# Attention weights turned by VectorE, a mask in the scores' tile shape, and queries and keys copied out of PSUM by ScalarE, with a new order of steps

## The chip, the cores and the metric

The kernel runs on one core of a Trainium2 chip. A core has a matrix engine (TensorE, PE in the profile, with PEld for its weight loads), VectorE (DVE), ScalarE (ACT), GpSimd (POOL) and a queue engine for DMAs (SyncE, SP). Each engine takes its instructions in order; semaphores tie them together. The metric is the device time in microseconds. The kernel before was run three times: 4847.99, 4833.86 and 4830.67 us, median 4833.86 us.

## The reference

The model is computed in float32 on 16 sequences of 256 tokens with 128 features. It has four parts in a row:

- latent attention (16 heads of 8), added to the stream;
- six layers of windowed attention with a feed-forward part; window 32, 16 heads of 64;
- a state-space layer (a scan over chunks);
- two layers of windowed attention with a feed-forward part; window 64, 8 heads of 64.

One layer of windowed attention, cut to what matters here:

```python
q, k, v = split(x @ Wqkv)                     # per head, 64 wide
q = l2norm(q) * q_scale ; k = l2norm(k) * k_scale
q = q * cos * scale + rotate_half(q) * sin * scale
k = k * cos / scale + rotate_half(k) * sin / scale
sim = einsum(q, [k of the window before, k of this window]) * 8.0
sim = where(mask, -max, sim)
out = softmax(sim) @ [v of the window before, v of this window]
x = x + out @ Wo
x = x + (a * gelu(gate)) @ W2 + b2            # a, gate = layernorm(x) @ W1 + b1
```

## The kernel before

The windowed layers are one class, Pipeline, used twice: W = 32 for the six layers and W = 64 for the two. The residual stream stays in SBUF as `k.y`, features on partitions. The work is cut into blocks of 128 tokens, 32 blocks per layer; two blocks make a sequence (a pair), and four blocks make a tile of 512 tokens for the feed-forward part. So the six-layer stage has 192 blocks, 96 pairs and 48 tiles.

What a block goes through, by step names. `project` (L791) multiplies y by Wqkv into PSUM (`pq`, `pk`, 128 tokens by 1024). `square` (L804, ACT) and `squares` (L847, DVE) give the norms. `cosine` (L817) and `sine` (L827), both on DVE, multiply the PSUM result by the tables into SBUF (`rot`, `t2`). `rotate` (L855, POOL) adds the two. `pair_newton` (L859, POOL) makes the reciprocal roots of a pair's norms in 13 small instructions, and `unit` (L874, POOL) applies them. `turn` (L881, PE) transposes to PSUM and `keep` (L888, ACT) copies to SBUF. `hide` (L970, PE) writes the mask into the bank of the scores as a product of two small matrices, `score` (L988, PE) adds q by k there in tiles of 64 rows by 32 columns. `maximum`, `subtract` (DVE), `exp` (ACT), `total`, `invert` (DVE) and `divide` (L1035, POOL) are the softmax. `turn_p` (L1040, PE) transposes the weights by 128x128 pieces and `keep_p` (L1046, ACT) copies them out.

For W = 32 the value and output matrices are folded into one (`wvo`), so the weights are applied to y itself. `turn_y` (L923) transposes the block of y, `keep_y` (L942, ACT) copies it, `spread` (L958) copies it by DMAs on SP's queue into four shifted windows `vc`, and `gather` (L1076, PE) multiplies windows by weights. `keep_u` (L1093, ACT) copies to `oT`, `pair_output` (L1103, PE) multiplies by `wvo` once per pair in four parts, and `pair_add` (L1115, DVE) adds to y. Steps named `ff_` are the feed-forward part, once per tile.

The order is written out by hand in PLAN32 and PLAN64 (L532, L549). An entry `name@lag` says that in round i the step is issued for block i - lag; the rounds run in `run` (L756), and each engine's queue gets its instructions in that order. So a waiting instruction holds everything that stands behind it on its engine. Before each round one piece of foreign work is issued: `rest`, the end of the stage before, and two hooks. PSUM is used as four double banks of 128x1024 float32, called q, s, t and o. The second string of a plan gives each tile its double bank; a new tile waits until the last user of that bank has been read.

## Time and profile before

The table is from the profile of one execution. The page gives its span, 4843.4 us, and no other time of its own; the span stands 0.2% above the median of the three runs.

| | value |
|---|---|
| span of the profiled execution | 4843.4 us |
| first stage, latent attention | until 440 us |
| six-layer stage | 440 to about 3740 us |
| state-space stage | until about 4080 us |
| two-layer stage | to the end |
| busy share PE / DVE / ACT / POOL | 94% / 70% / 57% / 68% |
| granted TensorE clock, mean | 0.975 |

In a line of a group, the shapes come first, then the number of instructions, the busy time in us and the mean duration of one in ns; behind the second bar stands the idle time of the engine just before them and what ended it. A line of the timeline begins with start and duration in us. A line about one source line gives the shortest, median and longest duration in ns. In the windows view a line gives the stretch, its length, the busy time of PE, PEld, DVE, ACT and POOL (with the number of instructions), the granted clock, the share of DMA and its rate. TensorE handles a float32 matrix product as two records.

### The profile page before, as it was taken

To read this page: it belongs to the slowest core of one execution; us is meant where nothing else is said; L and a number is where in the kernel's file an instruction comes from. 1 tells how busy PE (TensorE), PEld (TensorE's weight loads), DVE (VectorE), ACT (ScalarE), POOL (GpSimd) and SP (SyncE) were. 2 spreads that over 40 slices of the span, in tenths; PEclk is the share of its full clock that TensorE was granted. 3 is DMA by queue.
4 is the path that set the end of the run, shared out by engine and by line. 5 is a ranking of instruction groups with operands and counts; after the bars stand their busy time and mean duration, and the time that the engine had idled before them with its cause. 6 is when DMAs were issued, how large, how long until landed. Compare 5 with 4: busy or idle time off the path is not lost.

```text
span 4843.4 us, 121146 instructions
## 1 busy us (share of the span) xinstructions
PE 4566.5 (94%) x50834; PEld 3046.7 (63%) x50834; DVE 3371.6 (70%) x4050; ACT 2746.6 (57%) x3412; POOL 3302.7 (68%) x3603
## 2 busy tenths in 40 slices
PE   7896899999999999999999999999998998999998
PEld 4553566666666666666666666666665665566665
DVE  4664777777777777777777777777673775788774
ACT  3553465566656666566665666656664553566554
POOL 2444677777777777777777777777874354777774
PEclk9997999999999999999999999999998898999999
DMA  1111010001100010001000010000011000111111
GB/s 35 35 32 43 16 39 16 16 16 23 34 16 21 17 40 16 16 17 39 17 16 16 17 39 17 16 16 24 23 25 33 24 10 18 58 43 44 49 57 39
DMA packets 208039, 131.52 MB, mean 27 GB/s; under 512 B 61260, under 2 KB 179416, under 8 KB 207496
## 3 DMA queue, kind: packets, MB, share of 16 engines
q1 hardware_dynamic: 197096, 118.78, 9.9%
q8 instruction: 403, 6.60, 0.6%
q0 software_dynamic: 8704, 4.48, 0.5%
q14 instruction: 140, 1.15, 0.1%
q10 hardware_dynamic: 1696, 0.51, 0.0%
HBM read 29.65 MB, written 8.39 MB: 8 GB/s over the span
## 4 chain that ended last, share of the span: by engine, by line
PE 71%; DVE 16%; POOL 5%; ACT 4%; issue 2%; SPq 1%; DMA 0%; DVEq 0%; ACTq 0%; POOLq 0%
PE py L1111 13%; PE pq L796 7%; PE hid L1168 6%; PE u L1085 6%; PE scores L998 5%; PE pk L796 5%; PE tq L886 4%; DVE n L853 3%; PE tp L1044 3%; PE fy L1202 3%; PE tk L886 2%; DVE rotq L821 2%; PE st L383 2%; POOL rstd L116 1%; DVE rotk L821 1%
## 5 line engine op out<-in xcount | busy, mean ns | idle before, releaser
L1111 PE MATMUL py<-oT,wvo 128*128 128x256 f32 x3072 | 679.0, 379 | 1.2 <-ACT oT L1098 1.2
L1038 POOL TENSOR_TENSOR pr<-pr,rs 128x1024 f32<-128x1024 f32 x256 | 490.2, 1915 | 271.5 <-DVE rs L1033 231.8
L857 POOL TENSOR_TENSOR rotq<-rotq,t2q 128x1024 f32<-128x1024 f32 x256 | 605.6, 2366 | 36.1 <-DMA w<-in_L_ffn_W 23.6
L1111 PEld LDWEIGHTS py<-oT,wvo 128*128 128x128 f32 x3072 | 576.2, 190 | 76.0 <-ACT oT L1098 1.6
L1098 ACT COPY oT<-u 128x1024 f32<-128x1024 f32 x384 | 377.2, 1015 | 315.4 <-PE u L1085 306.9
L796 PE MATMUL pq<-wqkv,y 128*128 128x512 f32 x1024 | 493.1, 604 | 25.5 <-DMA wqkv<-in_L_ffn_Wqkv 14.0
L877 POOL TENSOR_TENSOR rotq<-rotq,rn 128x1024 f32<-128x1024 f32 x256 | 489.5, 1912 | 11.2
L101 DVE TENSOR_TENSOR y<-y,py 64x256 f32<-64x256 f32 x256 | 107.3, 419 | 525.0 <-PE py L1111 523.3
L821 DVE TENSOR_TENSOR rotq<-pq,tab 128x1024 f32<-128x1024 f32 x256 | 313.4, 1224 | 220.7 <-ACT sqq L807 169.5
L903 ACT COPY qT<-tq 128x1024 f32<-128x1024 f32 (+1 forms) x256 | 230.8, 902 | 412.1 <-PE tq L886 412.1
L857 POOL TENSOR_TENSOR rotk<-rotk,t2k 128x1024 f32<-128x1024 f32 x192 | 454.5, 2367 | 0.0
L998 PEld LDWEIGHTS scores<-kT,qT 64*32 64x32 f32 (+1 forms) x26624 | 321.4, 107 | 159.8 <-issue 96.7
L1029 DVE TENSOR_REDUCE rs<-pr 128x16 f32<-128x1024 f32 (+1 forms) x256 | 312.4, 1220 | 156.7 <-ACT pr L1022 151.9
L807 ACT ACTIVATE sqq<-pq 128x1024 f32<-128x1024 f32 x256 | 262.2, 1024 | 262.7 <-PE pq L796 244.9
L1085 PE MATMUL u<-prT,vc 64*128 64x256 f32 x3072 | 404.4, 394 | 2.3 <-DVE t2k L833 0.3
L998 PE MATMUL scores<-kT,qT 64*32 64x64 f32 (+2 forms) x26624 | 399.8, 224 | 4.7 <-ACT kT L903 2.8
L796 PE MATMUL pk<-wqkv,y 128*128 128x512 f32 x768 | 393.4, 601 | 0.0
L1168 PE MATMUL hid<-fxn,w 128*128 128x512 f32 (+1 forms) x768 | 388.3, 617 | 4.9 <-DVE ga L1190 2.7
L866 POOL TENSOR_SCALAR rn<-n 128x64 int32<-128x64 int32 (+1 forms) x128 | 30.5, 238 | 518.8 <-DVE n L853 518.8
L877 POOL TENSOR_TENSOR rotk<-rotk,rn 128x1024 f32<-128x1024 f32 x192 | 365.9, 1906 | 0.1
L1022 ACT ACTIVATE pr<-pr 128x1024 f32<-128x1024 f32 x256 | 270.6, 1057 | 135.3 <-DVE pr L1014 128.0
L1009 DVE TENSOR_REDUCE nm<-scores 128x16 f32<-128x1024 f32 (+1 forms) x256 | 311.9, 1218 | 21.0 <-PE scores L998 19.7
(285 smaller groups left out, 9772.0 us busy)
## 6 DMA issues: line engine op xcount, KB each, us to landing
vc<-vt SPq DMA_DIRECT2D x1152, 32.0 KB
vc<-vt SPq DMA_DIRECT2D x64, 256.0 KB
vc<-vt SPq DMA_DIRECT2D x96, 128.0 KB
vc<-vt SPq DMA_DIRECT2D x576, 16.0 KB
wqkv<-in_L_ffn_Wqkv SPq DMA_DIRECT2D x12, 512.0 KB
x<-xd SPq DMA_DIRECT2D x23, 256.0 KB
xd<-x SPq DMA_DIRECT2D x22, 256.0 KB
wo<-in_L_ffn_Wo SPq DMA_DIRECT2D x6, 512.0 KB
```

What stands on the lines that cost most here:

```text
L796: self.nc.tensor.matmul(pq[:, 512 * int(half) : 512 * int(half) + 512], self.k.y[:, b, c0 : c0 + P], L.wqkv[:, col : col + 512], start=Tru ...
L821: self.nc.vector.tensor_mul(rot.rearrange("p (w h) e -> p w h e", w=ways), self.get(n, "p" + group).rearrange("p (w h e) -> p w h e", w=wa ...
L857: self.nc.gpsimd.tensor_add(rot, rot, self.done(n, "t2" + group))
L877: self.nc.gpsimd.tensor_mul(rot, rot, rn.unsqueeze(2).to_broadcast(list(rot.shape)))
L998: self.nc.tensor.matmul(sc[ch * W : (ch + 1) * W, par, c, first : self.KS], qT[rows, c, ch * W : (ch + 1) * W], kT[rows, c, t0 - W + first ...
L1009: self.nc.vector.tensor_reduce(nm, self.get(n, "scores"), AX.X, ALU.max, negate=True)
L1029: self.nc.vector.tensor_reduce(rs, self.by_head(n), AX.X, ALU.add)
L1038: self.nc.gpsimd.tensor_mul(pr, pr, rs)
L1085: self.nc.tensor.matmul(pu[:, par, :, j, :], self.vc[n % 3][rows, ch, :], prT[rows, :, ch * W : (ch + 1) * W], start=True, stop=True,)
L1098: self.nc.scalar.copy(self.get(n - blk, "oT")[:, :, q0 : q0 + 64].rearrange("p (c i) q -> p i c q", i=2), self.done(n, "u" + half).rearran ...
L1111: self.nc.tensor.matmul(py, w[:, c, :], oT[:, c, :], start=(c == 0), stop=(c == last))
L1168: self.nc.tensor.matmul(pg[0:n, at : at + TT], L.w1[:, col : col + n], self.get(t, "fxn"), start=True, stop=True,)
```

## The change

Seven things change, the first four for W = 32 alone.

- `turn_p` and `keep_p` leave the plan. `shuffle` takes their place: one VectorE instruction that transposes each 32x32 block of the weights from SBUF to SBUF.
- `gather` follows that layout. Instead of eight products over 64 rows and 256 columns there are eight over 32 rows and 512 columns, two of them added up in PSUM for each window. The windows of y are read from `yt2`, two transposes of y, the second shifted by one window; `spread`, its DMAs and `vc` are gone.
- `hide` writes the mask with eight products of 64 rows by 32 columns instead of two of 64 rows by 128 columns.
- PLAN32 is new: other order, other lags (attention up to one round later, feed-forward up to three), and other double banks.
- `lift`, for both window sizes: ScalarE copies `pq` and `pk` to SBUF (`rot`, three buffers), and the PSUM bank is free. `square`, `cosine` and `sine` read that copy; `cosine` works in place. There is one buffer for squares instead of one each for q and k.
- PLAN64 gets `lift.q` ahead of `square.q`, and `sine.q` and `cosine.q` change places.
- `rest` and the hooks become an entry of the plan with a bank of their own; parts of `pair_output` and `ff_out` may come in any order; the tile `x` of the last layer shares buffers with `cen`.

```diff
 PLAN32 = (
-    project.q.0@0 project.q.1@0 project.k.0@0 ff_in.0.gate@11 invert@3 turn_y@0 square.q@0
-    cosine.q@0 project.k.1@0 sine.q@0 keep_y@0 turn.k@2 square.k@0 ff_center@9 ff_in.1.gate@12
-    cosine.k@0 ff_in.1.a@12 ff_mean@10 keep.k@2 sine.k@0 squares.q@0 hide@2 ff_in.0.a@11
-    score.0@2 ff_gelu.1@12 squares.k@0 score.1@2 ff_keep@10 ff_square@9 gather.0@4 divide@3
-    ff_var@10 gather.1@4 pair_newton@1 keep_u.0@4 ff_gate.1@12 spread@1 unit.q@1 score.2@2
-    ff_root@10 keep_u.1@4 ff_gelu.0@11 score.3@2 turn_p@3 pair_output.0.4@5 pair_output.1.4@5
-    ff_in.2.gate@12 ff_in.2.a@12 ff_out.0@12 rotate.q@0 keep_p@3 maximum@2 pair_output.2.4@5
-    pair_output.3.4@5 subtract@2 ff_gelu.2@12 unit.k@1 rotate.k@0 ff_gate.0@11 exp@2
-    ff_spread@10 ff_gate.2@12 turn.q@1 pair_add@5 total@2 keep.q@1 ff_out.1@12 ff_norm@10
-    ff_out.2@12 ff_add@12
+    turn.k@3 sine.q@1 keep.q@3 ff_mean@11 square.q@1 pair_add@7 ff_var@11 ff_in.1.a@12
+    ff_gate.2@14 keep.k@3 gather@5 rotate.k@2 squares.q@1 divide@4 hide@3 cosine.q@1
+    square.k@1 squares.k@1 score.0@3 score.1@3 rotate.q@1 keep_u.0@5 score.3@3 pair_newton@2
+    score.2@3 project.q.0@0 keep_u.1@5 project.q.1@0 maximum@3 ff_gelu.0@14 subtract@3
+    pair_output.0.4@6 ff_gelu.1@12 ff_in.2.gate@13 ff_out.0@15 rest@8 ff_keep@11
+    pair_output.3.4@6 ff_root@11 ff_in.2.a@13 lift.q@0 pair_output.1.4@6 sine.k@1 exp@3
+    ff_spread@11 shuffle@4 ff_gate.0@14 turn_y@0 total@3 ff_in.0.gate@13 project.k.0@0
+    keep_y@0 ff_gelu.2@13 ff_norm@11 project.k.1@0 ff_out.2@15 ff_out.1@15 cosine.k@1
+    unit.q@2 ff_gate.1@12 ff_center@10 ff_square@10 invert@3 turn.q@2 unit.k@2
+    ff_in.1.gate@11 lift.k@0 ff_in.0.a@13 ff_add@15 pair_output.2.4@6
-    pq:o pk:t tq:s tk:s tp:s scores:o yt:s norm:q hid0:q hid1:q hid2:t fy:q u0:s u1:t py:t
+    norm:q u1:s scores:t u0:o pq:o yt:o pk:t hid2:s hid0:q rest:t tq:o py:s hid1:q fy:s tk:t
...
+    def lift(self, n, group):
+        rot = self.new(n, "rot" + group, [P, 16, E], 3)
+        self.nc.scalar.copy(rot.rearrange("p h e -> p (h e)"), self.done(n, "p" + group))
+
     def square(self, n, group):
-        sq = self.new(n, "sq" + group, [P, 16, E], 1)
-        pq = self.get(n, "p" + group)
-        self.nc.scalar.activation(sq.rearrange("p h e -> p (h e)"), pq, AF.Square)
+        sq = self.work.tile([P, 16, E], F32, tag="sq", bufs=1, name=self.k.name("sq"))
+        self.live["sq" + group, n] = sq
+        self.nc.scalar.activation(sq, self.get(n, "rot" + group), AF.Square)
...
     def cosine(self, n, group):
         tab, ways = self.table(n, group, 0)
-        rot = self.new(n, "rot" + group, [P, 16, E])
+        rot = self.get(n, "rot" + group).rearrange("p (w h) e -> p w h e", w=ways)
         shape = [P, ways, 16 // ways, E]
-        self.nc.vector.tensor_mul(
-            rot.rearrange("p (w h) e -> p w h e", w=ways),
-            self.get(n, "p" + group).rearrange("p (w h e) -> p w h e", w=ways, e=E),
-            tab.unsqueeze(2).to_broadcast(shape),
-        )
+        self.nc.vector.tensor_mul(rot, rot, tab.unsqueeze(2).to_broadcast(shape))
...
     def turn_y(self, n):
-        self.nc.tensor.transpose(yt[:, 0:P], self.k.y[:, b, t0 : t0 + P], self.k.ident)
+        for i, first in enumerate((t0 - self.W, t0)):
+            self.nc.tensor.transpose(
+                yt[:, bass.ts(i, P)], self.k.y[:, b, first : first + P], self.k.ident
+            )
...
     def hide(self, n):
+        if self.W == 32:
+            for ch in range(self.NC):
+                for par in range(2):
+                    rows = slice(64 * par, 64 * par + 64)
+                    cols = slice(ch * self.W, (ch + 1) * self.W)
+                    self.nc.tensor.matmul(
+                        sc[cols, par],
+                        self.pick[rows, blk, cols],
+                        self.mask[rows, blk].unsqueeze(1).to_broadcast([64, self.NP, self.KS]),
+                        start=True,
+                        stop=True,
+                        skip_group_check=True,
+                    )
+            return
...
+    def shuffle(self, n):
+
+        prT = self.new(n, "prT", [P, 1024])
+        self.nc.vector.transpose(prT, self.done(n, "pr"))
...
-    def gather(self, n, half):
+    def gather(self, n):
+        prT = self.done(n, "prT").rearrange("p (h f w) -> p h f w", f=2, w=W)
+        vt = self.done(n, "yt2")
+        pus = [self.bank(n, f"u{i}").rearrange("p (k h w) -> p k h w", k=2, w=W) for i in range(2)]
+        for f in range(2):
+            for ch in range(self.NC):
+                rows = slice(ch * W, (ch + 1) * W)
                 self.nc.tensor.matmul(
-                    pu[:, par, :, j, :],
-                    self.vc[n % 3][rows, ch, :],
-                    prT[rows, :, ch * W : (ch + 1) * W],
-                    start=True,
-                    stop=True,
+                    pus[ch // 2][:, ch % 2],
+                    vt[rows, f, :],
+                    prT[rows, :, f, :],
+                    start=(f == 0),
+                    stop=(f == 1),
                 )
```

## The prediction

> **What bounds the kernel now.** I read the engine shares and slices of the page first, then the windows view cut by stage, then the groups of the middle window, and last, for the change itself, single stretches of the timeline.
>
> ```profile
> PE 4566.5 (94%) x50834; PEld 3046.7 (63%) x50834; DVE 3371.6 (70%) x4050; ACT 2746.6 (57%) x3412; POOL 3302.7 (68%) x3603
> 1500.00:2000.00 500.00, 493.67 (x6116) 337.54 (x6116) 366.29 (x384) 305.46 (x344) 377.62 (x368) 1.00 0.10 23
> ```
>
> The second line is 500 us from the middle of the six-layer stage (PE, PEld, DVE, ACT, POOL busy, then clock). TensorE is busy 493.67 of 500 us at full clock, and the output product, 32 records per pair of 128-token blocks, occurs 480 times: 15 pairs, so 33.3 us per pair and 16.67 per block. Per block that is PE 16.46, DVE 12.21, ACT 10.18, POOL 12.59 us. TensorE is the limit here; POOL and DVE are idle about a quarter of the time. The stage has 96 pairs, so 1 us per pair is 96 us.
>
> ```profile
> L1044 PE MATMUL tp<-ident,pr 128*128 128x128 f32 x240 | 32.7, 279 | 0.0
> L928 PE MATMUL yt<-ident,y 128*128 128x128 f32 x30 | 8.2, 273 | 0.0
> L821 DVE TENSOR_TENSOR rotk<-pk,tab 128x1024 f32<-128x1024 f32 x30 | 36.6, 1220 | 6.3 <-ACT sqk L807 5.8
> L853 DVE TENSOR_REDUCE n<-sqq 128x16 f32<-128x1024 f32 x30 | 36.3, 1209 | 0.0
> L857 POOL TENSOR_TENSOR rotq<-rotq,t2q 128x1024 f32<-128x1024 f32 x30 | 71.0, 2367 | 0.0
> L877 POOL TENSOR_TENSOR rotq<-rotq,rn 128x1024 f32<-128x1024 f32 x30 | 57.4, 1913 | 1.3
> L1048 ACT COPY prT<-tp 128x1024 f32<-128x1024 f32 x30 | 30.3, 1010 | 15.4 <-PE tp L1044 15.4
> ```
>
> The reader should see that the cosine and sine products of VectorE read one operand in PSUM (pq, pk) and one in SBUF (tab). After the change both lie in SBUF. Three places in this trace show what such an instruction does to GpSimd:
>
> ```profile
> L1038 POOL TENSOR_TENSOR pr<-pr,rs x256: 1893/1904/2427, 490.2 to 4797.1; 128x1024 f32<-128x1024 f32 x128
> 1801.10 2.43 POOL L1038 TENSOR_TENSOR pr<-pr,rs 128x1024 f32<-128x1024 f32 x1 [3.56 <-DVE sc L703]
> 1801.07 0.69 DVE L705 TENSOR_TENSOR tab<-rt,sc 128x512 f32<-128x512 f32 x1
> ...
> 1420.98 1.91 POOL L1038 TENSOR_TENSOR pr<-pr,rs 128x1024 f32<-128x1024 f32 x1
> 1422.84 2.17 POOL L877 TENSOR_TENSOR rotq<-rotq,rn 128x1024 f32<-128x1024 f32 x1
> 1421.21 2.04 DVE L732 TENSOR_SCALAR w<-w,c_ln_g 128x682 f32<-128x682 f32 x1
> ...
> 4057.64 0.73 DVE L1511 TENSOR_TENSOR y<-y,sz 128x256 f32<-128x256 f32 x1
> 4057.36 0.73 POOL L1477 TENSOR_TENSOR ce<-ce,cT 128x256 f32<-128x256 f32 x1 [2.48 <-ACT ce L1476]
> ```
>
> Line L705 multiplies two SBUF tensors. The division that starts beside it takes 2.43 us where the median is 1.90: it was held 0.52 us. Line L732 starts 0.23 us into a division, ends 0.36 us after it, and the next POOL instruction is held 0.27 us (2.17 against 1.90). L1511, two SBUF tensors, usually 0.42 us, takes 0.73: it ends 0.28 us after the POOL multiplication ends. These instructions exclude each other, whole instruction against whole instruction, first come first served. The 1.22 us products with a PSUM operand run beside POOL rows of 1.90 and 2.37 us without lengthening either.
>
> The Trainium skill, page "SBUF — State Buffer", section "SBUF: two separate sides", says it as a rule: VectorE with two SBUF inputs and GpSimd take one shared port pair as an exclusive lock for the whole instruction. The rows agree. By the rule each such product takes its full 1.22 us from POOL, 0.17 more than I take below, and the floor below would be 17.5 instead of 16.8 us.
>
> **The change, part by part (six-layer stage, per block).**
>
> *Weights turned by VectorE.* The PE transposes L1044 go: 32.7/30 = 1.09 us of PE busy time, one transpose of y comes (8.2/30 = 0.27, though starts move by only 0.11). The PSUM copy L1048 goes from ACT (1.01). VectorE gets one 32x32-block transpose of 128x1024. No row shows it. Bounds: 0.57 us (the shortest of the eight L732, 682 elements) and 2.4 us (twice a reduction). I take 1.21, the row L853, which also reads one SBUF tensor of 1024.
>
> *Value gather.* Before 16 records of 64 rows by 256 columns, 2.00 to 2.29 us in the timeline; after 16 records of 32 rows by 512. In the first stage 16 records of 32 rows by 256 columns start within 1.08 us; twice that is 2.16. Bounds 1.7 and 2.3; taken as no change. The copies of spread, 8 to 10 DMAs a block on SP's queue, vanish; nobody on the chain waited for them, so 0.
>
> *Mask in eight pieces of 64x32.* Two records now start 0.32 us before the scores. If the eight overlap like the scores (64 records in 0.77 us) nothing changes; if not, eight times 0.16 is +1.0. Taken 0.
>
> *Copies out of PSUM (lift).* ACT gets 2 x 1.01 and loses L1048: 10.18 + 2.02 - 1.01 + 0.12 (wider copy of y) = 11.3 us, under 16. The squares then read SBUF at 1.02 as before.
>
> *Sums.* PE 16.46 - 0.82 = 15.6; DVE 12.21 + 1.21 = 13.4; ACT 11.3; POOL 12.59. If nothing else happened, PE would stay the limit and the stage would gain 0.82 x 192 = 157 us.
>
> *The price of the two SBUF operands.* Four products per block (cosine and sine of q and k) now exclude POOL. A 0.69 us product starting 0.03 before a POOL instruction held it 0.52, so a 1.22 us one holds it about 1.05: 4 x 1.05 = 4.2. POOL busy plus held is 12.59 + 4.2 = 16.8 us, already more than the present 16.67, with no idle time at all. The 13 small Newton instructions (0.24 to 0.37 us) start 0.41 apart, 5.3 us per pair against 4.15 busy: another 0.6 per block is lost between them: 17.4. On its side VectorE waits for whatever POOL is executing, up to 2.37 us.
>
> *One pair laid out by hand*, from the new step order, VectorE at 1.13 us from start to start and POOL at 2.32 (rotate) and 1.86 (unit, divide). Even block: sine.q 0 to 1.1; rotate.k to 3.4; cosine.q, which waited, to 4.5; divide to 6.3; rotate.q to 8.6; sine.k, asked for at 7.9, to 9.7; Newton from 9.7, 5.3 long and pushed by cosine.k and the next sine.q (1.0 each), to 17.0; unit.q to 18.9. PE's turn.q waits for it (PE by itself would be there at 14.4), then the last quarter of the output product, to 21.5. VectorE stands at pair_add until then, with squares, cosine and all of the odd block queued behind it: pair_add to 22.5, squares.q 23.7, cosine.q after POOL's divide 25.0 to 26.1, rotate.q 28.4, unit.q 30.3, sine.k, held back since 29.5, to 31.4, transpose and total to 33.7, cosine.k 34.8, invert 35.1, and the next pair begins. So 35.1; the feed-forward steps of every second pair (0.66 and 1.5 us of VectorE) add 0.4, and some eight hand-overs between engines of 0.06 add 0.5: 36.0 us against 33.3. That is 2.7 x 96 = +259 us. PE's 0.82 saving is inside this: it turns into waiting.
>
> *Two-layer stage* (46 divisions, one per block, between 4200 and 4700 us: 10.9 us a block; POOL is busy 8.2 and PE 10.5 of it). Only two products per block meet POOL. The sine now runs against the division, and the cosine waits for that division, so maximum and subtract come up to 1.9 us later; PE reaches pair_output 1.0 after subtract today. Between 0 and 3.8 (two waits of 1.9); I take 0.6 per block, the part of 1.9 beyond that 1.0, with odd blocks partly covered: +38.
>
> *Fill and drain.* Attention lags grow by one, the feed-forward by three. One more filling round of some 18 us in which PE works 10 (first output product at 533, five rounds after 440) is +8; the drain's three extra rounds hold only short feed-forward chains, +4. The rest and hook steps move behind the scores' bank for some ten rounds: within that.
>
> Sum: 259 + 38 + 12 = +309. The profiled span is 4843.4 us, 0.2% above the median of 4833.86; I add to the median: 5143, rounded to **5140 us**.
>
> **Rivals.**
> 1. *POOL's floor is reached* (17.0 to 17.4 per block): the two engines interleave so that no wait spreads to pair_add. For it: POOL has about 4 us idle per pair today that a new order could fill. Against: VectorE is in order. 0.5 x 192 plus 40 gives about 4970.
> 2. *Lock step*: even blocks take POOL's 15.6 + 4.2, odd ones VectorE's 14.3 + 4 waits of 1.1, 38.5 a pair: +500 and 50, 5380. A transpose of 2.4 us, or one that excludes POOL as well, leads here too.
> 3. *The other side: faster.* The exclusion costs POOL under 0.7 us per product, for instance because waits fall on Newton's gaps; the decisive point is POOL plus held time under PE's 15.6, so under 0.75 each. Then PE limits: -157 + 50 = about 4730. Against: 0.52 us for a product of half the size.
> 4. *No visible change*: the same between these, 4834.
>
> **How the numbers follow.** Chances: forecast (its own range 5030 to 5280) 0.54, rival 1 0.18, rival 2 0.15, rival 3 0.10, rival 4 0.03. The range takes rival 1 nearly whole and reaches to rival 2: 4900 to 5370. A difference of 0.5% is about what a measurement of this kernel can tell from none: slower 0.87, same 0.03, faster 0.10.
>
> **What would show it.** Right: the cosine and sine groups of VectorE rise from 1.22 to about 2 us mean with maxima above 3; POOL's rotate, unit and divide groups rise by 0.3 to 0.7 us; PE's busy share in the middle falls from 99% to about 90%, with idle time of turn.q put down to POOL and of pair_add on VectorE to PE; pairs of 35 to 37 us. Wrong: POOL rows stay at 1.90 and 2.37, or the pair falls to 31.5 us with PE at 98%. A transpose row far from 1.21, or a gather above 2.3, would move the sum by 192 times the difference.

## The result, and the profile after

The changed kernel takes 5236.84 us, the median of four runs (5227.58 to 5254.59); the kernel before, run beside it on the same chip, takes 4835.22 us. The ratio is 1.083, with a 95% interval of 1.081 to 1.086: slower by about 400 us. The profiled execution has a span of 5252.6 us, 409 us more than the 4843.4 of before.

To place the difference I cut both spans at the first and last record of the projections of each windowed stage. What the six-layer stage still does after its last projection is thus counted with the state-space stage. The pair time is the mean over pairs 10 to 80, read from the output product (32 records a pair).

| | before | after | difference |
|---|---|---|---|
| until the first projection | 439.9 | 442.3 | +2 |
| six-layer stage | 3207.6 | 3497.3 | +290 |
| state-space stage | 429.2 | 426.1 | -3 |
| two-layer stage | 685.6 | 804.3 | +119 |
| tail | 81.1 | 82.4 | +1 |
| one pair in the six-layer stage | 33.63 | 36.70 | +3.07 |

The engine shares of the page after:

```profile
PE 4559.9 (87%) x50642; PEld 2922.2 (56%) x50642; DVE 3906.2 (74%) x4242; ACT 3000.0 (57%) x3672; POOL 3843.0 (73%) x3600
```

TensorE was 94% busy and is 87% busy. Two stretches of 500 us in the middle of the six-layer stage, in the windows view of after (busy time of PE, PEld, DVE, ACT, POOL, then the granted clock):

```profile
1500.00:2000.00 500.00, 442.84 (x5475) 289.43 (x5474) 388.51 (x376) 298.12 (x330) 407.28 (x333) 0.95 0.03 7
2000.00:2500.00 500.00, 446.56 (x5529) 290.34 (x5528) 402.13 (x384) 309.71 (x344) 419.17 (x343) 0.97 0.03 7
```

No engine is full any more. PE stands at 89%, where it stood at 99%, and VectorE and POOL stand at 80% and 84%. In the second stretch there are 500 / 36.70 x 2 = 27.2 blocks, so POOL is busy 15.4 us per block (12.6 before) and idle 3.0 (4.1 before). The chain of work that ended last, by engine, says the same; the first line is that of before, the second that of after:

```profile
PE 71%; DVE 16%; POOL 5%; ACT 4%; issue 2%; SPq 1%; DMA 0%; DVEq 0%; ACTq 0%; POOLq 0%
DVE 31%; PE 30%; POOL 24%; issue 8%; ACT 5%; SPq 1%; DMA 0%; POOLq 0%; DVEq 0%; ACTq 0%
```

Before, PE held 71% of that chain. Now three engines hand it to each other. The groups of the stretch from 2000 to 2500 us, with busy time and mean ns of one between the bars:

```profile
L860 POOL TENSOR_TENSOR rotk<-rotk,t2k 128x1024 f32<-128x1024 f32 x28 | 73.4, 2622 | 28.9 <-DVE rs L1054 28.9
L880 POOL TENSOR_TENSOR rotk<-rotk,rn 128x1024 f32<-128x1024 f32 x28 | 66.3, 2367 | 0.0
L1059 POOL TENSOR_TENSOR pr<-pr,rs 128x1024 f32<-128x1024 f32 x28 | 66.0, 2359 | 0.0
...
L880 POOL TENSOR_TENSOR rotq<-rotq,rn 128x1024 f32<-128x1024 f32 x28 | 58.5, 2089 | 1.2
L1111 PE MATMUL u<-prT,yt 32*128 32x512 f32 x432 | 58.4, 614 | 0.5 <-DVE ga L1224 0.5
...
L836 DVE TENSOR_TENSOR t2k<-rotk,tab 128x1024 f32<-128x1024 f32 x28 | 49.7, 1774 | 0.0
L836 DVE TENSOR_TENSOR t2q<-rotq,tab 128x1024 f32<-128x1024 f32 x28 | 40.9, 1459 | 0.2
L829 DVE TENSOR_TENSOR rotq<-rotq,tab 128x1024 f32<-128x1024 f32 x27 | 40.1, 1486 | 0.0
...
L829 DVE TENSOR_TENSOR rotk<-rotk,tab 128x1024 f32<-128x1024 f32 x28 | 39.4, 1407 | 0.0
...
L889 PE MATMUL tq<-ident,rotq 128*128 128x128 f32 x224 | 36.4, 316 | 38.0 <-POOL rotq L880 38.0
L1064 DVE STREAM_TRANSPOSE prT<-pr 128x1024 f32<-128x1024 f32 x28 | 34.5, 1233 | 0.0
...
L873 POOL TENSOR_SCALAR nt<-nt 128x64 f32<-128x64 f32 x42 | 25.9, 617 | 3.7
```

Read it against the lines of before, and against three more of them, from the same stretch of that kernel:

```profile
L886 PE MATMUL tq<-ident,rotq 128*128 128x128 f32 x240 | 31.5, 274 | 0.7 <-ACT prT L1048 0.6
...
L101 DVE TENSOR_TENSOR y<-y,py 64x256 f32<-64x256 f32 x30 | 12.6, 420 | 76.4 <-PE py L1111 76.2
...
L870 POOL TENSOR_SCALAR nt<-nt 128x64 f32<-128x64 f32 x45 | 11.0, 244 | 3.9
```

The products of cosine and sine (L829, L836), 1.22 us before, take 1.41 to 1.77. POOL's division (L1059), 1.90 before, takes 2.36; unit of k (L880, rotk) 2.37 against 1.91; rotate of k (L860) 2.62 against 2.37. The third of Newton's small instructions (L873, L870 before), 0.24 us before, takes 0.62 on average. TensorE's transposes of q (tq) wait 38.0 us for POOL, against 0.7 us in all before. The new transpose of the weights (L1064) takes 1.23 us, and the gather 58.4 us in 27 blocks, 2.16 per block.

How the lengthening comes about is seen in single instructions. First VectorE's part of the timeline of after, then POOL's:

```profile
2010.06 2.74 DVE L829 TENSOR_TENSOR rotq<-rotq,tab 128x1024 f32<-128x1024 f32 x1
...
2016.23 1.27 DVE L836 TENSOR_TENSOR t2k<-rotk,tab 128x1024 f32<-128x1024 f32 x1
2017.43 1.23 DVE L1064 STREAM_TRANSPOSE prT<-pr 128x1024 f32<-128x1024 f32 x1
```

```profile
2009.82 1.90 POOL L1059 TENSOR_TENSOR pr<-pr,rs 128x1024 f32<-128x1024 f32 x1
...
2016.52 1.10 POOL L873 TENSOR_SCALAR nt<-nt 128x64 f32<-128x64 f32 x1
2017.70 0.32 POOL L874 TENSOR_TENSOR rn<-rn,nt 128x64 f32<-128x64 f32 x1
2018.09 0.29 POOL L871 TENSOR_TENSOR nt<-rn 128x64 f32<-128x64 f32 x1
```

The cosine is issued at 2010.06, 0.24 us into a division that ends at 2011.72, and ends 1.08 us after it: it waited for the rest of the division. At 2016.23 VectorE comes first, and the small Newton instruction that starts at 2016.52 ends only after the product, 1.10 us instead of 0.24. The transpose of the weights at 2017.43 lies over the Newton instructions at 2017.70 and 2018.09 and lengthens neither.

### The profile page after: what moved, and what is told of

It is laid out like the page before. It is cut to its first block, busy times and chain, and to the rows that moved or that the text cites. A ratio compares the mean times of both kernels' runs of the same rounds, so it can differ in the third digit from the quotient of the medians.

```text
span 5252.6 us, 116843 instructions
## 1 busy us (share of the span) xinstructions
PE 4559.9 (87%) x50642; PEld 2922.2 (56%) x50642; DVE 3906.2 (74%) x4242; ACT 3000.0 (57%) x3672; POOL 3843.0 (73%) x3600
## 3 DMA queue, kind: packets, MB, share of 16 engines
q0 software_dynamic: 8704, 4.48, 0.5%
## 4 chain that ended last, share of the span: by engine, by line
DVE 31%; PE 30%; POOL 24%; issue 8%; ACT 5%; SPq 1%; DMA 0%; POOLq 0%; DVEq 0%; ACTq 0%
PE py L1140 5%; DVE rotq L829 5%; POOL rotq L860 5%; DVE n L856 5%; POOL rotq L880 5%; POOL nt L873 3%; DVE t2k L836 3%; PE tq L889 3%; DVE pr L1035 3%; DVE nm L1030 3%; POOL nt L872 3%; POOL nt L871 2%; DVE rs L1050 2%; POOL rn L874 2%; PE u L1111 2%
## 5 line engine op out<-in xcount | busy, mean ns | idle before, releaser
L860 POOL TENSOR_TENSOR rotq<-rotq,t2q 128x1024 f32<-128x1024 f32 x256 | 603.2, 2356 | 321.3 <-DVE rotq L829 303.9
L1140 PE MATMUL py<-oT,wvo 128*128 128x256 f32 x3072 | 777.1, 411 | 3.9 <-ACT oT L1124 3.3
L1140 PEld LDWEIGHTS py<-oT,wvo 128*128 128x128 f32 x3072 | 636.3, 210 | 140.3 <-issue 42.2
L1059 POOL TENSOR_TENSOR pr<-pr,rs 128x1024 f32<-128x1024 f32 x256 | 603.2, 2356 | 136.1 <-DVE rs L1054 96.5
L860 POOL TENSOR_TENSOR rotk<-rotk,t2k 128x1024 f32<-128x1024 f32 x192 | 504.4, 2627 | 206.5 <-DVE rs L1054 193.9
L800 PE MATMUL pq<-wqkv,y 128*128 128x512 f32 x1024 | 513.6, 625 | 75.9 <-ACT oT L1124 58.4
L856 DVE TENSOR_REDUCE n<-sq 128x16 f32<-128x1024 f32 x448 | 543.5, 1213 | 34.7 <-ACT sq L815 31.3
L889 PE MATMUL tq<-ident,rotq 128*128 128x128 f32 x2048 | 318.9, 307 | 283.4 <-POOL rotq L880 283.4
L880 POOL TENSOR_TENSOR rotq<-rotq,rn 128x1024 f32<-128x1024 f32 x256 | 544.8, 2128 | 11.1
L889 PEld LDWEIGHTS tq<-ident,rotq 128*128 128x128 f32 x2048 | 268.1, 157 | 453.9 <-POOL rotq L880 377.1
L880 POOL TENSOR_TENSOR rotk<-rotk,rn 128x1024 f32<-128x1024 f32 x192 | 454.1, 2365 | 0.0
L829 DVE TENSOR_TENSOR rotq<-rotq,tab 128x1024 f32<-128x1024 f32 x256 | 438.5, 1713 | 6.7
L1111 PE MATMUL u<-prT,yt 32*128 32x512 f32 x3072 | 418.7, 615 | 8.0 <-DVE ga L1224 6.6
L810 ACT COPY rotq<-pq 128x1024 f32<-128x1024 f32 x256 | 258.4, 1009 | 262.0 <-PE pq L800 244.4
```

What stands on the lines that cost most here:

```text
L800: self.nc.tensor.matmul(pq[:, 512 * int(half) : 512 * int(half) + 512], self.k.y[:, b, c0 : c0 + P], L.wqkv[:, col : col + 512], start=Tru ...
L829: self.nc.vector.tensor_mul(rot, rot, tab.unsqueeze(2).to_broadcast(shape))
L856: self.nc.vector.tensor_reduce(sums, self.done(n, "sq" + group), AX.X, ALU.add)
L860: self.nc.gpsimd.tensor_add(rot, rot, self.done(n, "t2" + group))
L880: self.nc.gpsimd.tensor_mul(rot, rot, rn.unsqueeze(2).to_broadcast(list(rot.shape)))
L889: self.nc.tensor.transpose(pt[:, cut], rot[:, cut], self.k.ident)
```

## The experiments

Two kinds were made. The first take the exclusion of VectorE and POOL away or do single parts of the change. The second look for a version that keeps the gain. All are compared with runs of the kernel before on the same chip, whose medians were 4838 to 4846 us. One operand, half, and one operand, keep first, leave the rotary tables out of the computation in part or in whole: they show what something costs and are no versions to use.

| kernel | median us | ratio, 95% interval | six layers | two layers | pair |
|---|---|---|---|---|---|
| after | 5236.84 | 1.083 [1.081, 1.086] | 3497.3 | 804.3 | 36.70 |
| one operand | 4641.03 | 0.958 [0.956, 0.960] | 2973.6 | 723.0 | 30.99 |
| half | 4770.92 | 0.985 [0.983, 0.986] | 3099.8 | 723.0 | 32.22 |
| lift alone | 5802.5 | 1.198 [1.196, 1.200] | 4002.5 | 849.2 | 42.14 |
| shuffle alone | 4942.28 | 1.020 [1.019, 1.022] | 3309.0 | 685.4 | 34.72 |
| turn last | 5136.57 | 1.061 [1.058, 1.064] | 3381.6 | 804.9 | 35.24 |
| half from PSUM | 4904.39 | 1.013 [1.010, 1.015] | 3282.3 | 685.2 | 34.32 |
| no lift | 5117.21 | 1.058 [1.055, 1.060] | 3490.9 | 685.1 | 36.44 |
| sine between | 5124.09 | 1.058 [1.056, 1.060] | 3497.3 | 685.2 | 36.59 |
| lift first | 4998.93 | 1.032 [1.030, 1.034] | 3382.7 | 685.1 | 35.39 |
| lift first, turn last | 5029.97 | 1.039 [1.037, 1.040] | 3404.0 | 685.2 | 35.65 |
| squares later | 5098.21 | 1.051 [1.048, 1.054] | 3459.6 | 684.9 | 36.25 |
| one operand, keep first | 4722.06 | 0.975 [0.973, 0.977] | 2971.4 | 805.6 | 30.94 |

**One operand: the exclusion taken away.** Order, banks, buffers and the number of instructions stay as after; the four products are replaced by an instruction of VectorE with one operand in SBUF and nearly the same length, a transpose, which leaves the rotary tables out.

```diff
     def cosine(self, n, group):
+            flat = self.get(n, "rot" + group).rearrange("p h e -> p (h e)")
+            self.nc.vector.transpose(flat, flat)
+            return
...
     def sine(self, n, group):
+            flat = [v.rearrange("p h e -> p (h e)") for v in (t2, rot)]
+            self.nc.vector.transpose(*flat)
+            return
```

> The changed kernel, but cosine and sine (both stages) are VectorE 32x32-block transposes of the same 128x1024 tile, 1.23 us each in the profile of the changed kernel, with one SBUF operand instead of two. The rotary tables are left out of the computation; order, banks, lags, copies and instruction counts stay. Theory A (VectorE products with two SBUF operands and POOL instructions exclude each other): POOL rows fall back to 1.90 and 2.36 us, pairs of blocks in the six-layer stage fall from 36.8 to 31.5 to 33 us, the two-layer stage from 804 us to 690 to 720, total 4680 to 4800 us. Rival B (the new order with its longer lags and other banks costs the time): pairs stay at 36 to 37 us, total 5150 to 5240. Rival C (the added ScalarE copy sits on the path): also near 5200, with ACT copies named as what ended PE's idle time.

4641 us: not only is the whole loss gone, this kernel, without the tables, is 4.2% faster than before, a little under the range expected (4680 to 4800). The window from 2000 to 2500 us and three groups of it:

```profile
2000.00:2500.00 500.00, 498.30 (x6539) 327.31 (x6537) 429.60 (x452) 360.39 (x404) 410.19 (x395) 1.00 0.03 7
```

```profile
L868 POOL TENSOR_TENSOR rotk<-rotk,t2k 128x1024 f32<-128x1024 f32 x33 | 78.2, 2371 | 35.1 <-DVE rs L1062 35.1
...
L888 POOL TENSOR_TENSOR rotk<-rotk,rn 128x1024 f32<-128x1024 f32 x33 | 62.9, 1906 | 0.0
...
L831 DVE STREAM_TRANSPOSE rotk<-rotk 128x1024 f32<-128x1024 f32 x33 | 40.7, 1234 | 0.0
```

POOL's rows are back at 2.37 and 1.91, though VectorE's stand-ins take 1.23 us each, as long as the products. PE is full again (498.30 of 500) at the full clock. So the loss belongs to the exclusion: 5252.6 - 4642.5 = 610 us between the two spans, of which 524 in the six-layer stage and 81 in the two-layer stage.

**Half the exclusion.** The same replacement for k alone in the six-layer stage (for both in the two-layer stage); the products of q stay.

```diff
     def cosine(self, n, group):
+        if self.W == 64 or group == "k":
+            flat = self.get(n, "rot" + group).rearrange("p h e -> p (h e)")
+            self.nc.vector.transpose(flat, flat)
+            return
```

> The same replacement for the key products alone in the six-layer stage, and for both products in the two-layer stage (tables left out there); cosine and sine of the queries keep two SBUF operands. Theory A: half of the exclusion is left, about 2.1 us per block, so POOL busy plus held is 14.7 us and under PE's 15.6; pairs of 33 to 35 us, total 4800 to 5000 us, between the full replacement and the changed kernel. Rival B or C: within 40 us of the changed kernel less whatever the two-layer stage gives, 5080 to 5200.

4771 us, 1.5% faster than before and just under what was expected (4800 to 5000); the pair of 32.22 is under its range too. The products of q alone cost 32.22 - 30.99 = 1.23 us per pair, those of k on top of them 36.70 - 32.22 = 4.48. Its window and three groups:

```profile
2000.00:2500.00 500.00, 483.60 (x6313) 307.09 (x6312) 443.32 (x432) 347.94 (x390) 431.90 (x381) 1.00 0.01 3
```

```profile
L888 POOL TENSOR_TENSOR rotq<-rotq,rn 128x1024 f32<-128x1024 f32 x32 | 60.9, 1902 | 1.3
...
L833 DVE TENSOR_TENSOR rotq<-rotq,tab 128x1024 f32<-128x1024 f32 x31 | 57.5, 1854 | 0.0
...
L881 POOL TENSOR_SCALAR nt<-nt 128x64 f32<-128x64 f32 x47 | 11.5, 244 | 4.1
```

PE is still 97% busy, though the cosine of q takes 1.85 us, longer than after. These two exclusions per block are mostly covered by PE's work; all four are not. Whether the number decides or the place was not separated: with q's products alone Newton's instruction stays at 244 ns and the unit of q at 1902, both of which stand ahead of turn.q; with k's products added they take 617 and 2089. A kernel that keeps k's products alone was not run.

**Lift alone.** The order and the banks of before, with only the copy out of PSUM put in, for both window sizes (and sine and cosine changing places, since the cosine works in place). The copy has two buffers here and three in after.

```diff
-    ... turn_y@0 square.q@0
-    cosine.q@0 project.k.1@0 sine.q@0 keep_y@0 turn.k@2 square.k@0 ...
-    cosine.k@0 ff_in.1.a@12 ff_mean@10 keep.k@2 sine.k@0 ...
+    ... turn_y@0 lift.q@0 square.q@0
+    sine.q@0 project.k.1@0 cosine.q@0 keep_y@0 turn.k@2 lift.k@0 square.k@0 ...
+    sine.k@0 ff_in.1.a@12 ff_mean@10 keep.k@2 cosine.k@0 ...
```

> The kernel before with its own order and banks, and only the copy out of PSUM added (lift; square, cosine and sine read SBUF). Theory A: slower than before by at least the floor, POOL busy plus held 16.8 to 17.4 us a block, and by more through waits: 5000 to 5350 us; POOL rows lengthen as in the changed kernel. Rival B (order): 4800 to 4870. Rival C (ScalarE's copy): 4850 to 5000 with POOL rows at 1.90 and 2.36 us.

5802 us, 20% slower than before and outside what was expected. Groups of the window from 2000 to 2500 us:

```profile
L855 POOL TENSOR_TENSOR rotq<-rotq,t2q 128x1024 f32<-128x1024 f32 x24 | 62.5, 2604 | 0.0
...
L831 DVE TENSOR_TENSOR t2q<-rotq,tab 128x1024 f32<-128x1024 f32 x23 | 56.2, 2442 | 22.7 <-ACT rotq L806 19.5 <-POOL rotk L875 1.4 <-POOL rotk L855 1.4
```

In the old order the sine of q takes 2.44 us on average, twice its own length: it is lengthened nearly every time, and it stands behind ScalarE's copy as well (19.5 of its 22.7 us of idle time before). But not all of the 20% is the exclusion. A line of the waits of the whole run:

```profile
PE scores L996 <- ACT kT L901: 330.0, 190, 2.8
```

Before, this wait was 2.8 us in the whole run. On ScalarE lift.k stands ahead of keep.k, the copy that the scores need, and lift.k waits 282 us itself for turn.k on TensorE, which is the last to read the buffer that it writes. So a part of the loss belongs to the place of the copy and to its two buffers, and how much the exclusion makes in this order was not separated. What the run shows is that the copy costs more in the old order than the whole change does in the new one; that the new order does not cause the loss is shown by one operand.

**Shuffle alone.** The order of before with the weights turned by VectorE, the new gather and the new mask; no copy out of PSUM.

```diff
-    score.0@2 ... gather.0@4 divide@3
-    ff_var@10 gather.1@4 pair_newton@1 keep_u.0@4 ff_gate.1@12 spread@1 unit.q@1 score.2@2
+    score.0@2 ... divide@3
+    ff_var@10 gather@4 pair_newton@1 keep_u.0@4 ff_gate.1@12 unit.q@1 score.2@2
...
-    pair_output.3.4@5 subtract@2 ff_gelu.2@12 unit.k@1 ...
+    pair_output.3.4@5 subtract@2 shuffle@3 ff_gelu.2@12 unit.k@1 ...
```

> The kernel before with the weights turned by VectorE, the new gather and the mask in eight pieces, but without the copy out of PSUM and in the order of before (shuffle after subtract, one gather step where its second half stood). Theory A: none of this meets POOL, PE saves 0.82 us a block as the sum of the prediction says, total 4670 to 4760 us, pairs of 31.5 to 32.5 us. Rival D (the turn itself costs: VectorE at 13.4 us a block becomes a limit, or the gather over 32 rows is slower): 4800 us and more.

4942 us, 2% slower than before, where a gain was expected. It is near what the rival named, 4800 us and more. PE waits more (window from 2000 to 2500 us, and a line of the waits of the whole run: what was waited for, us in total, times, longest):

```profile
2000.00:2500.00 500.00, 475.24 (x5942) 294.19 (x5942) 389.12 (x402) 270.38 (x303) 364.20 (x349) 1.00 0.03 7
```

```profile
ACT oT L1122 <- PE u L1109: 481.1, 192, 8.8
```

The gather in one piece adds two windows into each bank, so the first half is finished later than in two pieces, and ScalarE waits 481 us for it, 2.5 us per block, with its whole queue behind; before, it waited 307 us for its two pieces. That this wait is what PE's 25 idle us in 500 come from was not tested. Nor does PE's busy time fall in this order: 475.24 us for 28.8 blocks is 16.5 per block, as before. The transposes of the weights are gone, but the gather, in its one place here, takes 80.7 us in 29 blocks, 2.8 per block, against 2.1 before and 2.16 in after. So the saving on TensorE does not come by itself. It came, 15.4 us per block, in the new order with the copy and without the exclusion (one operand).

**Turn last.** After, with one step moved: turn.q at the end of the round, behind the last quarter of the output product.

```diff
-    unit.q@2 ff_gate.1@12 ff_center@10 ff_square@10 invert@3 turn.q@2 unit.k@2
-    ff_in.1.gate@11 lift.k@0 ff_in.0.a@13 ff_add@15 pair_output.2.4@6
+    unit.q@2 ff_gate.1@12 ff_center@10 ff_square@10 invert@3 unit.k@2
+    ff_in.1.gate@11 lift.k@0 ff_in.0.a@13 ff_add@15 pair_output.2.4@6 turn.q@2
```

> The changed kernel with one step moved: turn.q stands behind the last quarter of the output product at the end of the round. PE then finishes the product without waiting for POOL's unit.q, and pair_add on VectorE no longer inherits that wait. If the waits reach the end through this loop (theory A as laid out by hand in the prediction), pairs fall from 36.7 by 1 to 3 us and the total to 4950 to 5150 us. If the pair is set by the exclusion alone, each engine serving its sum, or by another loop, less than 0.5 us a pair changes: 5190 to 5280.

5137 us, within what was expected; a pair falls by 1.46 us. Two lines of the waits page of after, then the same two of this kernel:

```profile
DVE y L102 <- PE py L1140: 634.5, 109, 9.6
PEld tq L889 <- POOL rotq L880: 377.1, 122, 11.2
```

```profile
PEld tq L889 <- POOL rotq L880: 184.1, 121, 11.2
...
DVE y L102 <- PE py L1140: 161.8, 102, 6.2
```

Both waits fall, the first line's by three quarters, the second's by a half. So part of the loss did go through the loop that the layout by hand drew: POOL late for turn.q, turn.q in front of the output product, VectorE standing at pair_add. What moving turn.q away takes off is half of the 3.07 us per pair that the change costs on the whole, and a quarter of the 5.71 that the exclusion costs; the rest remains without it.

**Half from PSUM.** The cosine reads PSUM again and runs in the round of its projection, ahead of the copy; only the sine reads the copy. The two-layer stage is as before. To find room, the copy, the turned weights and the turned queries have one buffer each.

```diff
-    ... squares.q@1 divide@4 hide@3 cosine.q@1
+    ... squares.q@1 divide@4 hide@3
-    ... ff_gelu.0@14 subtract@3
+    ... ff_gelu.0@14 subtract@3 cosine.q@0
-    ... ff_out.1@15 cosine.k@1
+    ... ff_out.1@15 cosine.k@0
...
     def cosine(self, n, group):
-        rot = self.get(n, "rot" + group).rearrange("p (w h) e -> p w h e", w=ways)
+        rot = self.new(n, "rot" + group, [P, 16, E], 3 if self.W == 32 else 2)
-        self.nc.vector.tensor_mul(rot, rot, tab.unsqueeze(2).to_broadcast(shape))
+        self.nc.vector.tensor_mul(
+            rot.rearrange("p (w h) e -> p w h e", w=ways),
+            self.get(n, "p" + group).rearrange("p (w h e) -> p w h e", w=ways, e=E),
+            tab.unsqueeze(2).to_broadcast(shape),
+        )
```

> The whole computation again. Six-layer stage of the changed kernel, but cosine reads the PSUM bank at lag 0 just before it is freed, into a tile of its own; sine and squares read the copy (copies, transposed weights and queries in one buffer to make room). So two of the four products have two SBUF operands. The two-layer stage is that of before, without the copy. Theory A: pairs near the 32.2 us that the half replacement gave, 32 to 34, two-layer stage 686 us instead of 804, total 4730 to 4880, faster than the kernel before or near it. Rival E (VectorE or the bank held longer costs what the exclusion gave): above 4900.

4904 us, more than expected. Two of the four products exclude POOL, as in the kernel called half, though here it is the two sines and there the two of q; the pair is 34.32 against 32.22 there. The waits of the whole run:

```profile
ACT rawq L810 <- DVE rotq L834: 466.1, 190, 6.3
...
DVE n L867 <- ACT sq L820: 282.4, 249, 2.1
```

Two readers of one PSUM bank are kept in order in these kernels: the copy of q waits for the cosine, 2.5 us per block, and that of k another 383 us in the whole run. And since the cosine no longer stands between the two sums of squares, VectorE waits 282 us in 249 times, 1.13 us on average, most of it at the second sum until ScalarE has filled the one buffer of squares again. The first of these waits reaches TensorE: from 2000 to 2500 us it is idle 42.2 us, and 32.0 of them end when the copy has read pq or pk and so freed the bank. How the 2.1 us between the two pairs divide was not tested further.

**No lift.** The new order with both products read from PSUM, in the round of their projections, and no copy. Beside what the cut shows, three feed-forward steps move ahead of turn_y, the turned weights and queries have one buffer each, and the two-layer stage is as before.

```diff
-    turn.k@3 sine.q@1 keep.q@3 ff_mean@11 square.q@1 pair_add@7 ff_var@11 ff_in.1.a@12
+    turn.k@3 keep.q@3 ff_mean@11 pair_add@7 ff_var@11 ff_in.1.a@12
-    ff_gate.2@14 keep.k@3 gather@5 rotate.k@2 squares.q@1 divide@4 hide@3 cosine.q@1
+    ff_gate.2@14 keep.k@3 gather@5 rotate.k@1 squares.q@1 divide@4 hide@3
-    ... subtract@3
+    ... subtract@3 cosine.q@0 sine.q@0
```

> The whole computation. As the kernel with half of the products on PSUM, but no copy at all in the six-layer stage: cosine, sine and squares read PSUM at lag 0, rotate.k comes one round earlier, two feed-forward steps move ahead of turn_y to cover the longer hold of the banks. No product has two SBUF operands. Theory A: POOL rows back at 1.90 and 2.36 us; pairs between 31 and 33.5 us, the rest being PE's waits for the banks that two VectorE products hold 2.3 us; total 4660 to 4850. Rival E: the banks cost more than that, above 4900.

5117 us, nearly as slow as after in the six-layer stage (36.44 against 36.70 per pair), with the four products no longer excluding POOL. Three groups of the window from 2000 to 2500 us, and waits of the whole run:

```profile
L861 POOL TENSOR_TENSOR rotk<-rotk,t2k 128x1024 f32<-128x1024 f32 x28 | 66.2, 2363 | 139.6 <-DVE rs L1055 89.5 <-DVE t2k L837 50.1
...
L890 PE MATMUL tk<-ident,rotk 128*128 128x128 f32 x216 | 29.7, 282 | 40.7 <-ACT sqk L811 37.8 <-issue 2.8
...
L933 PE MATMUL yt<-ident,y 128*128 128x128 f32 x54 | 11.0, 286 | 16.3 <-ACT sqq L811 16.3
```

```profile
ACT sqq L811 <- DVE t2q L837: 732.5, 189, 8.3
...
DVE nm L1031 <- PE scores L1020: 558.3, 217, 6.4
```

POOL's rows are unlengthened, yet POOL, ScalarE and VectorE all wait, and so does PE: of its 58.5 idle us in these 500, 54.1 end when ScalarE's square has read pk or pq, whose banks (t and o) tk and yt take next. The square itself waits for VectorE's sine. This is the rival in the expectation, a bank held longer by two products of VectorE. In this order the copy is what frees the banks early, and it can't simply be left out.

**Three orders more, and one.** All start from half from PSUM. Sine between moves sine.k between the two sums of squares, to fill that wait. Lift first does that too and puts the copies ahead of the cosines. The third also moves turn.q to the end of the round.

```diff
-    square.k@1 squares.k@1 score.0@3 ...
+    square.k@1 sine.k@1 squares.k@1 score.0@3 ...
-    ... lift.q@0 pair_output.1.4@6 sine.k@1 exp@3
+    ... lift.q@0 pair_output.1.4@6 exp@3
```

> The half-PSUM version (4904, pair 34.32) with one step moved: sine.k now stands between squares.q and squares.k, so that VectorE has work while ScalarE refills the single buffer of squares. In the half-PSUM version VectorE waited 282 us there (n <- sq), 1.12 us per block. Theory A (VectorE's in-order queue and what it excludes set the pair): the wait nearly vanishes, a pair falls by about 1 us, 4790 to 4860. If the other waits set the pair (ScalarE's copies behind the cosines, 466 us): 4890 to 4910.

> The same, and ScalarE's copy out of PSUM (lift) stands ahead of VectorE's cosine of the same bank, so that the cosine follows the copy in place of the copy following the cosine. The 466 us in which ScalarE waited for cosines goes; VectorE may wait for a copy of 1.0 us where it comes early. Theory A: POOL's rows are unchanged (only the two sines exclude it), pair 32.2 as with half the exclusion before, 4700 to 4790. Rival: the copy waits for the same bank's end and VectorE, in order, waits longer than ScalarE did: 4860 or more.

> The same as the version with the copy first, with turn.q moved to the end of the round, behind the last quarter of the output product. Theory A: where POOL is the late one at turn.q this takes up to 1.5 us from a pair as it did with full exclusion (36.70 to 35.24); with half the exclusion POOL is rarely late, so 0 to -60 us against the version before it.

5124, 4999 and 5030 us: in none did what was hoped for come, and all are slower than half from PSUM; for lift first the rival had said 4860 or more. Waits of the kernel with the copy first:

```profile
POOL pr L1070 <- DVE rs L1065: 494.7, 144, 9.6
DVE rotk L834 <- ACT rawk L810: 361.8, 192, 6.1
```

The wait for cosines is gone, but VectorE now waits 362 us for a copy of k. And POOL waits 495 us for VectorE's reciprocal of the sums (284 us in half from PSUM). Turn.q moved to the end, which gained 1.46 us a pair in after, costs 0.26 here.

The last move puts squares.k behind maximum, and Newton's steps behind it:

```diff
-    square.k@1 squares.k@1 score.0@3 ... score.3@3 pair_newton@2
+    square.k@1 score.0@3 ... score.3@3
-    ... project.q.1@0 maximum@3 ff_gelu.0@14 subtract@3 cosine.q@0
+    ... project.q.1@0 maximum@3 squares.k@1 pair_newton@2 ff_gelu.0@14 subtract@3 cosine.q@0
```

> The half-PSUM version (4904, pair 34.32) with squares.k moved behind maximum, and Newton's steps behind it on POOL; the products stay where they are. VectorE then takes the scores' maximum in the 1.12 us in which ScalarE refills the buffer of squares, 282 us of waiting in the whole run. Theory A (VectorE's own chain sets the pair): 1 us of a pair, 4800 to 4850, beside the kernel before. Rival: the place of every VectorE step sets when POOL can work, and Newton that starts later holds unit and turn.q: slower than 4904, as the move of sine.k was (5124).

5098 us: the rival's direction. One wait of its waits page:

```profile
DVE nm L1041 <- PE scores L1030: 448.5, 217, 6.0
```

In half from PSUM this wait was 46 us: the maximum now mostly comes before the scores are there. The copy's wait for the cosine of q has grown as well, from 466 to 612 us. No order tried with all four products in place was faster than before.

**One operand, keep first.** In the kernel with one operand the two-layer stage still takes 723.0 us against 685.6 before, with no exclusion left. There, ScalarE's lift.q stands ahead of its copy keep.q.

```diff
-    ... turn.q@2 lift.q@0 square.q@0 turn_p@4
+    ... turn.q@2 turn_p@4
-    ... invert@3 sine.q@0 ff_center@9 keep.q@2
+    ... invert@3 ff_center@9 keep.q@2 lift.q@0 square.q@0 sine.q@0
```

> The kernel with transposes of one operand (4641; the tables are left out of q and k, as there), with one thing changed in the two-layer stage: lift.q, square.q and the product of the sine are issued behind keep.q instead of ahead of it. In that kernel the two-layer stage still took 723.0 us against 685.6 before, with no exclusion left in it. Theory A: TensorE's values wait there for ScalarE's copy qT, 29.8 us in 500 (43 blocks; before 3.2 in 46), 0.62 us per block, because lift.q stands ahead of that copy on ScalarE: 64 blocks make 40 us, so the stage falls to 680 to 695 and the time to about 4605. Rival: the 37 us come from the changed places of sine and cosine or from the copy's work itself: the stage stays at 715 to 725 and the time at 4640.

The wait that was aimed at does vanish. A line of the waits from 4000 to 4500 us, in one operand, then two in this kernel:

```profile
PE values L922 <- ACT qT L914: 29.8, 32, 1.6
```

```profile
DVE t2q L841 <- ACT rotq L810: 71.1, 38, 2.9
...
PE values L922 <- ACT qT L914: 2.9, 10, 0.3
```

But the sine now waits 1.9 us per block for the copy, and the stage rises to 805.6 us. Neither expectation held. So where these three steps stand is worth 83 us there, and neither place reaches 685. Whether the wait of values makes the 37 us stays open.

## Why the prediction was right, and where it was off

*The sign and its cause* were right: the slowdown is the exclusion of the four products and POOL. One operand shows it directly: its stand-ins have the length, the place and the buffers of the products and differ in being transposes that read one operand from SBUF instead of two. The Trainium skill, page "SBUF — State Buffer", section "SBUF: two separate sides", names two SBUF inputs on VectorE, beside a two-port mode of it, as a condition of the lock. The runs agree: with one such input POOL's rows are 1.91 and 2.37 us, with two up to 2.37 and 2.62. Of the signs named, the pair and PE's 89% came, and so did the waits. The products rise to 1.41 to 1.77 us, with maxima of 2.9 to 3.0, and not to about 2; the division and the unit of k rise by about 0.45, the rotation of k by 0.25, the unit of q by 0.18, and the rotation of q, which often starts when its cosine has just ended, not at all.

*Durations of the parts.* The weights' transpose was taken at 1.21 us and takes 1.23. The gather was to stay within 1.7 to 2.3 us and takes 2.16. The mask was costed at nothing: its eight records are busy 11.1 us in 27 blocks, the two of before 11.7 us in 30. VectorE's sum was 13.4 us per block: 402.13 / 27.2 = 14.8, less 1.3 of lengthened products, is 13.5. ScalarE's 11.3 is 309.71 / 27.2 = 11.4. TensorE's 15.6 is seen where nothing disturbs it, in one operand: 498.30 / 32.3 blocks = 15.4.

*The hold of 1.05 us per product* was mis-sized (4.2 us per block). POOL is busy 15.4 us per block, 2.8 over the 12.59 of before: 0.70 per product. The four products themselves lose another 1.3 us per block waiting for POOL. The two share the conflicts: who comes second pays, and the prediction booked nearly all of it on POOL. It reached POOL's period all the same, because POOL's idle time is 3.0 us per block and not the 0.6 between Newton's instructions: 15.4 + 3.0 = 18.4 per block, against 18.0 from the layout. That the hold taken too large and the idle time taken too small offset each other is luck.

*The pair of 36.0 us* measured 36.70. Against 33.63 before (the prediction had read 33.3), that is 3.07 x 96 = 295 us where 259 stood. The loop through turn.q, the output product and pair_add is real: taking it away gave 1.46 us of the pair. That pair_add waits for PE was named as its sign, and is a poor one: VectorE stood there 76.4 us of 500 before as well (80.0 after). The 38.0 us of PE behind POOL at turn.q are the better sign.

*The two-layer stage* is the term that failed: +38 predicted, +119 measured. The exclusion makes 81 of it (804.3 against 723.0), 1.27 us per block. From 4500 to 5000 us its two products take 2.31 and 1.59 us, 1.5 us per block more than their 1.22 and 1.21 of before. The prediction let 1.0 us of each delay be absorbed by the time that PE takes to reach the output product and took 0.6 us per block; whether it is this slack that did not appear was not tested. The other 37 us go with the copy and the places of sine and cosine, since the kernels with the old two-layer order and no copy take 685; the prediction counted nothing for that. *Fill and drain* had +12; all that is left over is -5.

The terms, against the 409 us between the spans: 259 should have been 295, 38 should have been 119, 12 should have been -5. The total of 309 was 100 too low, and the median with it.

*The rivals.* Rival 1's floor for POOL, 17.0 to 17.4 us per block, was not reached: the block takes 18.4. Rival 3's condition was POOL plus held time under PE's 15.6 us per block, under 0.75 us per product. It was met, if narrowly: 0.70 and 15.4. And the kernel is 8% slower. So the point from which it decides was wrong: a busy sum under the bound does not help where the waits fall on a chain through all three engines, and VectorE's own 0.3 us per product was not in that sum. Without the exclusion the time is 4641, below that rival's 4730: the pair of 30.99 is PE's own 15.4 per block with almost no idle time, where the rival only took 0.82 off the 16.67 of before. Lock step (38.5 us a pair) was not reached in the new order; in the old order (lift alone) the pair of 42.14 passed it, though with ScalarE's copy in the way as well.

*What lies outside.* PE's busy time per block is 446.56 / 27.2 = 16.4 us after, 1.0 more than in one operand for the same instructions (the transposes tq 316 ns against 272), at a granted clock of 0.97 against 1.00. In the stretches shown here the clock is 1.00 where PE is busy 475 us or more of 500 and 0.95 to 0.97 where it is busy 443 to 447, so it goes with the waiting; how much of the loss is this slower clock was not separated.

The Trainium skill, page "VectorE: DVE Perf Modes", section "Rules for kernel authors", advises for elementwise work on a matrix product's output either to accept the PSUM source or to copy to SBUF first where many operations follow. Here three operations follow each copy, and in the old order the copy, with sine and cosine changing places, cost 20%, part of it through ScalarE. In the new order the exclusion that comes with the copy cost 610 us, and leaving the copy out was no way out either (no lift, 5117 us). So where the other operand is in SBUF and POOL is busy, many operations alone do not decide for the copy.

## What to carry to other kernels

Before moving an operand of VectorE from PSUM to SBUF, ask whether the instruction then has two SBUF operands, and what POOL does at that time: a single pair of such rows in the timeline shows the price of one meeting (1.05 us by the prediction's estimate, 0.70 on POOL and 0.3 on VectorE as measured on average). What the meetings cost in time is another matter: those of q's products hide behind the bound engine (1.23 us a pair), all four do not (5.71), so a busy sum below the bound is no promise; a layout by hand, in order, through every engine that waits, came within 0.7 us of the pair. In an order that is tuned to this degree one moved step of about 1 us was worth between 2% less (turn.q) and 4.5% more (sine.k) of the whole time.

## What was not expected of the hardware

- A 32x32-block transpose of 128x1024 float32 takes 1.23 us on VectorE and doesn't hold POOL, nor is it held: 1230 to 1245 ns over all 192, between products that range from 1.2 to 3.0.
- POOL's instructions of 0.24 us on 128x64 are held like the large ones: up to 1.32 us. Thirteen of them in a row are no free gap for VectorE's products, as one that meets a product can cost POOL nearly the whole of it.
- The cost of the exclusion is not shared out evenly: of 5.71 us per pair, q's two products per block cost 1.23 and k's two, on top of them, 4.48. Whether that is the number or the place of k's products was not separated.
